# Cross-attention of a gated block on one core: scores, sums and values as eight small products side by side, with the softmax sums spread by DMA

## The chip, the core and the metric

The kernel runs on one core of one Trainium2 chip. The metric is the device time of one execution in microseconds (us). Times of whole runs are medians of several executions; everything said of single instructions comes from one profiled execution. TensorE (PE) does the matrix products, VectorE (DVE) and ScalarE (ACT) the elementwise work, GpSimd (POOL) some small elementwise work, and SyncE's queue (SP) issues every DMA of this kernel, in order.

## The reference, cut to what matters

There are 8 batches of 512 tokens with 512 features, and 64 context tokens per batch. Each batch passes through a cross-attention with 16 heads of 32 features, then through a feed-forward net with ternary weights.

```python
def xattn(hs, ctx, mask):                     # hs: layernorm(x), ctx: 64 tokens
    q, k, v = proj(hs, Wq, bq), proj(ctx, Wk, bk), proj(ctx, Wv, bv)   # 16 heads of 32
    s = clip(einsum('bhsd,bhtd->bhst', q, k) / sqrt(32), -50, 50)
    s = clip(where(attend, s, -1e4), -50, 50)
    p = softmax(s); p = p / (p.sum(-1) + 1e-8)
    c = einsum('bhst,bhtd->bhsd', p, v)        # heads side by side again
    d = rs * (c @ Wo.T + bo)
    return layernorm(d) * ln_gamma + ln_beta

x = x + tanh(g_xattn) * xattn(layernorm(x), ctx, mask)
x = x + tanh(g_ffn) * ffn(layernorm(x))        # ffn: silu(gate) * val, then out;
                                               # rows quantised to 8 bits, weights to -1, 0, 1
```

## The kernel before

Activations of the attention are 32-bit floats. A batch is cut into four token tiles of 128 (`ST`) and four feature chunks of 128 (`DC`); a chunk holds four heads. For each batch the loop at the end of `common_path` runs, chunk by chunk:

- `queries(b, o)`: four accumulating products (L236) give 128 query features of all 512 tokens, and ACT writes them to `qT` with the bias (L241).
- `scores(b, o)`: two products (L259), one for each pair of heads. The keys `kp` lie with zeros in the places of the other head, so that one product of 64 rows gives 2 heads x 64 context tokens on 128 partitions and 512 tokens along the row. ACT takes the exponential of both (L265).
- `values(b, o)`: eight products (L282). Here the probabilities are the stationary operand, 128 tokens at a time, and `vp` streams with 66 columns: 32 value features and a column of ones for each of two heads. So a softmax sum comes out beside the values, on the token's own partition. DVE takes the reciprocal (L289) and multiplies (L290) into `ctok`, which has tokens on partitions.
- `ctx_T(b, o)`: four transposes (L303) and a copy on ACT (L304) turn `ctok` into `cT`, with features on partitions, which `project_out` (L321) needs as its stationary operand.

Then come, per token tile, `project_out` with its bias, statistics and scaling on DVE (L326 to L330), and the transposes of the next batch's layernorm (`ln1`, L227, copied by ACT at L228).

The feed-forward tiles of earlier batches are set between these steps: `ffn_mid` computes half of a 128-token tile into the four PSUM banks of `psum4` (L539 for the bias rows, four products of 32 rows on four bands of the array; L544 for gate and value), ACT takes Silu (L550) and DVE multiplies (L551). `ffn_quant` finds the row maximum on DVE (L559), scales on ACT (L568), rounds on DVE (L569) and transposes through the DMA (L571). `ffn_out` (L580) multiplies by the output weights. The buffers `hq` and `hqT` hold one tile, in two halves. All other products share the four PSUM banks of `psum`. In batches 0 and 1 no feed-forward tile is there yet; between the steps stand the weights' preparation instead (`weights_step`: magnitudes L397 on ACT, ternary values L429 and L430 on DVE, each from a chunk `wraw` loaded by DMA; of `wraw` there are four buffers). After batch 7 nine tiles of the feed-forward net are left, and run alone.

Tile code is recorded in program order and then ordered for every engine by a scheduler, so that steps interleave; at run time each engine and the SP queue go through their own list in that order, and one that waits holds all that is behind it.

Of the kernel before, what the change touches and what calls it, by code (L numbers as in the profile page):

```python
# [9 lines left out]
F32 = mybir.dt.float32  # L10
# [7 lines left out]
P = 128  # L18
# [9 lines left out]
def common_path(  # L28
# [50 lines left out]
    psum = ctx.enter_context(tc.tile_pool(name="psum", bufs=4, space=bass.MemoryType.PSUM))  # L79
    psum4 = ctx.enter_context(tc.tile_pool(name="psum4", bufs=4, space=bass.MemoryType.PSUM))  # L80

    def bank():
        return psum.tile([P, NW], F32, tag="bank", name="bank")

# [12 lines left out]
    nc.gpsimd.memset(nmagic, -MAGIC)  # L97


    kp = const.tile([P, DC, B, 2, T], F32, name="kp")  # L100
    vtok = const.tile([P, CT, D], F32, name="vtok")

    vp = []
    for i in range(2):
        v = const.tile([P, NH // 2, 2, HD + 1], F32, name=f"vp{i}")
        nc.gpsimd.memset(v, 0.0)
        for hh in range(2):

            nc.gpsimd.memset(v[hh * T : (hh + 1) * T, :, hh, HD : HD + 1], 1.0 + 1e-8)
        vp.append(v)  # L110
    kv = ExitStack()
    kvp = kv.enter_context(tc.tile_pool(name="kv", bufs=1, side="right"))
    cT_in = kvp.tile([P, DC, B * T], F32, name="cT_in")
# [41 lines left out]
    attend_f = const.tile([P, B], F32, name="attend_f")  # L155
    most = const.tile([P, B], F32, name="most")

    par = const.tile([P, 2], F32, name="par")
    for q in range(2):
        nc.vector.tensor_reduce(  # L160
            par[:, q : q + 1],
            ident.rearrange("p (a q d) -> p q a d", q=2, d=HD)[:, q],
            AX.XY, ALU.add,
        )
    bkp = const.tile([P, 2, DC], F32, name="bkp")
    for q in range(2):
        nc.vector.tensor_scalar(bkp[:, q, :], bk_sb, par[:, q : q + 1], None, ALU.mult)

    def constants():
        nc.vector.tensor_copy(attend_f, mask_i)  # L170
        nc.vector.tensor_scalar(attend_f, attend_f, 0.5, None, ALU.is_gt)
# [16 lines left out]
    rs = const.tile([P, 2], F32, name="rs")  # L188

    mvall = const.tile([P, B * ST, 2], F32, name="mvall")  # L190
    ksum = const.tile([P, 2 * DC], F32, name="ksum")
    nok = const.tile([P, B], F32, name="nok")

    def rsqrt(dst, var, n=1):
# [37 lines left out]
    def queries(b, o):  # L232
        hT = st_[b, "hT"]
        ps = bank()
        for c in range(DC):
            nc.tensor.matmul(  # L236
                ps, wq_sb[:, c, o * P : (o + 1) * P], hT[:, c, :],
                start=(c == 0), stop=(c == DC - 1),
            )
        qT = work.tile([P, S], F32, tag="qT", name="qT", bufs=2)  # L240
        nc.scalar.activation(qT, ps, AF.Identity, bias=bq_sb[:, o : o + 1])  # L241
        st_[b, "qT", o] = qT

    def pair_up(b):

        src = vtok[(b % 2) * T : (b % 2 + 1) * T, b // 2, :].rearrange(
            "p (n h d) -> p n h d", h=2, d=HD
        )
        for hh in range(2):
            nc.gpsimd.tensor_copy(vp[b % 2][hh * T : (hh + 1) * T, :, hh, 0:HD], src[:, :, hh, :])  # L250

    def scores(b, o):

        qT = st_[b, "qT", o]
        pr = work.tile([P, 2, S], F32, tag="prob", name="prob", bufs=2)
        both = bank(), bank()
        for j, ps in enumerate(both):
            rows = slice(j * 2 * HD, (j + 1) * 2 * HD)
            nc.tensor.matmul(  # L259
                ps, kp[rows, o, b, :, :].rearrange("p q t -> p (q t)"), qT[rows, :],  # L260
                start=True, stop=True,
            )
        for j, ps in enumerate(both):

            nc.scalar.activation(  # L265
                pr[:, j, :], ps, AF.Exp, scale=esc[:, b : b + 1], bias=esh[:, b : b + 1]
            )
        st_[b, "pr", o] = pr

    def values(b, o):  # L270

        pr = st_[b, "pr", o]
        if o == 0:
            st_[b, "rden"] = work.tile([P, DC, 2, 2, 4], F32, tag="rden", name="rden", bufs=2)
        ctok = work.tile([P, ST, P], F32, tag="ctok", name="ctok", bufs=2)
        for half in range(2):
            ps = bank()
            pc = ps[:, : 4 * 2 * (HD + 1)].rearrange("p (t n d) -> p t n d", t=2, d=HD + 1)
            for i in range(2):
                t = half * 2 + i  # L280
                for j in range(2):
                    nc.tensor.matmul(  # L282
                        pc[:, i, 2 * j : 2 * j + 2, :],
                        pr[:, j, t * P : (t + 1) * P],
                        vp[b % 2][:, 2 * o + j, :, :],
                        start=True, stop=True,
                    )
            rden = st_[b, "rden"][:, o, half, :, :].unsqueeze(3)
            nc.vector.reciprocal(rden, pc[:, :, :, HD : HD + 1])  # L289
            nc.vector.tensor_tensor(  # L290
                ctok[:, half * 2 : half * 2 + 2, :].rearrange("p t (n d) -> p t n d", d=HD),
                pc[:, :, :, 0:HD],
                rden.to_broadcast([P, 2, 4, HD]),
                ALU.mult,
            )
        st_[b, "ctok", o] = ctok

    def ctx_T(b, o):
        ctok = st_[b, "ctok", o]
        cT = work.tile([P, S], F32, tag="cT", name="cT", bufs=DC)  # L300
        ps = bank()
        for t in range(ST):
            nc.tensor.transpose(ps[:, t * P : (t + 1) * P], ctok[:, t, :], ident)  # L303
        nc.scalar.copy(cT, ps)  # L304
        st_[b, "cT", o] = cT

    def check_sums(b):

        r = st_[b, "rden"].rearrange("p o h t n -> p (o h t n)")
        ok = work.tile([P, DC * 2 * 2 * 4], F32, tag="ok", name="ok", bufs=1)  # L310
        nc.vector.tensor_scalar(ok, r, most[:, b : b + 1], None, ALU.is_le)
        nc.vector.scalar_tensor_tensor(
            ok, r, 2e-22, ok, ALU.is_ge, ALU.mult, accum_out=nok[:, b : b + 1]
        )
# [281 lines left out]
                start=(c == 0), stop=(c == DC - 1),  # L596
            )
    for o in range(DC):
        for q in range(2):
            nc.scalar.activation(  # L600
                kp[:, o, :, q, :], kbanks[o].rearrange("p (b t) -> p b t", t=T), AF.Identity,
                scale=par[:, q : q + 1], bias=bkp[:, q, o : o + 1],
                accum_out=ksum[:, 2 * o + q : 2 * o + q + 1],
            )
    constants()
    for t in range(ST):
        ln1(0, t)
# [11 lines left out]
    stage = staging.enter_context(tc.tile_pool(name="stage", bufs=1, side="right"))  # L619
    pair_up(0)  # L620
    ternary_load("gate", gate_w, DC)
    nc.sync.dma_start(out=wo_sb, in_=wo.rearrange("(c p) o -> p c o", p=P))
    bcast(out_b, ob_bc)
    load_x(1)

    tiles = [(f, i) for f in range(B) for i in range(ST)]
    done = {"in": 0, "mid": 0, "out": 0}

    def feed_in():

        if done["in"] < len(tiles):
            ffn_in(*tiles[done["in"]])
            done["in"] += 1

    def feed(step):

        n = done["mid"]
        if step % 2 == 0:
            ffn_mid(*tiles[n], step // 2)
            return  # L640
        if step == 3:
            if n:
                ffn_out(*tiles[n - 1])
            ffn_quant(*tiles[n])
            done["mid"] += 1

    def weights_step(b, step):

        for call in {
# [15 lines left out]
        }.get((b, step), []):  # L665
            call[0](*call[1:])

    for b in range(B):


        if b > 1:
            ffn_stats(b - 2)
        if b:
            pair_up(b)
        if 0 < b < B - 1:
            load_x(b + 1)
        queries(b, 0)
        for o in range(DC):
            fed = (b == 2 and o > 1) or (b > 2 and o != 1)
            scores(b, o)  # L680
            if fed:
                feed(0)
                values(b, o)
            if o + 1 < DC:
                queries(b, o + 1)
            if not fed:
                values(b, o)
            if fed:
                feed(1)
                feed(2)  # L690
            if b > 1 and o:
                feed_in()
            ctx_T(b, o)
            if fed:
                feed(3)
            weights_step(b, o)
        if b == 0:
            sum_bounds()
        check_sums(b)
        if b + 1 < B:  # L700
            ln1_stats(b + 1)
        for t in range(ST):
            project_out(b, t)
            if b > 1:
                feed(t)
            if b + 1 < B:
                ln1(b + 1, t)
            weights_step(b, DC + t)
        add_delta(b)
        if b == 0:  # L710
            nc.vector.tensor_scalar(ob_bc, ob_bc, tg[:, 1:2], None, ALU.mult)
        if b == 1:
            nc.vector.tensor_copy(unit, gw)
            nc.vector.tensor_scalar(unit[:, 2:3], unit[:, 2:3], tg[:, 1:2], None, ALU.mult)
            staging.close()
            fp = ctx.enter_context(tc.tile_pool(name="fp", bufs=1, side="right"))
        if b > 1:
            feed_in()
        if b == B - 1:
            verdict()  # L720
    ffn_stats(B - 2)
    while done["mid"] < len(tiles):
        if tiles[done["mid"]] == (B - 2, 0):
            ffn_stats(B - 1)
        feed(0)
        feed_in()
        for step in range(1, 4):
            feed(step)
    ffn_out(B - 1, ST - 1)


@with_exitstack
def general_path(
# [576 lines left out]
```

## Time and profile before

| | us |
|---|---|
| median of 3 runs (lowest, highest) | 831.27 (828.74, 832.45) |
| the profiled execution | 836.41 |
| its span, from first to last instruction | 834.4 |
| start until the first query product, keys and values for all batches | 39.7 |
| batch 0 / batch 1, without feed-forward work (39.7 to 94.2, 94.2 to 150.3) | 54.5 / 56.1 |
| batch 2, in which the feed-forward work starts (150.3 to 245.0) | 94.7 |
| each of batches 3 to 6 | 92.2 to 92.4 |
| batch 7, without a next batch's layernorm (614.2 to 700.0) | 85.8 |
| feed-forward tiles alone (700.0 to the end) | 134.4 |

A batch is counted here from its first query product to that of the next. The profile's page gives busy shares by engine; since the parts of the kernel have different limits, the windows by batch say more than the mean.

### The profile page before, as it was taken

The page shows a single profiled execution, that of the slowest core. Times are in us where ns is not written, and L with a number is a line of the kernel's source. Part 1 is how long each engine was busy: PE and PEld are TensorE (multiplying, and loading weights), DVE is VectorE, ACT ScalarE, POOL GpSimd, SP SyncE. Part 2 cuts the span into 40 slices and gives each one's busy share as a digit, 9 for nine tenths or more (in the row PEclk, how much of TensorE's full clock was granted, in tenths as well). Part 3 has the DMA queues.
Part 4 walks back from the last instruction along what each step waited for, and adds up shares of the span by engine and source line. Part 5 has one row for each costly group of instructions (what it writes and reads, how often), then busy time and mean ns, then how long its engine had stood idle before and what let it go on. Part 6 is the DMA issues. An engine that isn't in the chain of part 4 may idle for free. (4 is left out here: it accounts for less than half of the span.)

```text
span 834.4 us, 9194 instructions
## 1 busy us (share of the span) xinstructions
PE 790.5 (95%) x3274; PEld 371.6 (45%) x3274; DVE 558.3 (67%) x1105; ACT 353.5 (42%) x435; POOL 136.3 (16%) x185
## 2 busy tenths in 40 slices
PE   7999999798999999999999999999999999999994
PEld 3445454343444544444445444444444443334441
DVE  2637787978588377765688367756786468876662
ACT  2274367334335452455344453455244442343341
POOL 1500301243013021212113021211121000300000
PEclk9997999889999999999999999999999999999998
DMA  8745041002221123222222041222222122243432
GB/s 283 237 198 202 0 162 66 1 19 39 57 57 34 38 69 45 51 64 57 57 57 60 11 102 21 49 57 58 44 45 51 32 57 45 44 83 64 88 76 55
DMA packets 106358, 59.15 MB, mean 71 GB/s; under 512 B 91712, under 2 KB 91712, under 8 KB 105280
## 3 DMA queue, kind: packets, MB, share of 16 engines
q1 hardware_dynamic: 106304, 58.49, 27.3%
q8 instruction: 27, 0.44, 0.2%
q14 instruction: 27, 0.22, 0.1%
HBM read 28.06 MB, written 8.39 MB: 44 GB/s over the span
## 5 line engine op out<-in xcount | busy, mean ns | idle before, releaser
L551 DVE SCALAR_TENSOR_TENSOR h<-four,sgv,gate 128x512 f32<-128x512 f32 x128 | 93.9, 745 | 120.5 <-PE four L544 86.4
L544 PEld LDWEIGHTS <-xqT 128*128 128x128 bf16 x1024 | 94.4, 99 | 133.0 <-issue 33.5
L550 ACT ACTIVATE gate<-four,sgv 128x512 f32<-128x512 f32 x128 | 86.1, 685 | 135.0 <-PE four L544 132.1
L544 PE MATMUL four<-gate_tern,xqT 128*128 128x512 fp8e4 x512 | 137.0, 385 | 0.3 <-DMA xqT<-xq 0.3
L544 PE MATMUL four<-val_tern,xqT 128*128 128x512 fp8e4 x512 | 133.6, 383 | 0.0
L236 PE MATMUL bank<-hT,wq_sb 128*128 128x512 f32 x256 | 124.1, 629 | 5.8 <-ACT hT L228 4.9
L580 PE MATMUL bank<-out_tern,hqT 128*128 128x512 fp8e4 x512 | 117.3, 383 | 6.4 <-DMA hqT<-hq 6.4
L568 ACT ACTIVATE h<-h,magic,h_s 128x1024 f32<-128x1024 f32 x64 | 75.9, 1233 | 104.4 <-DVE h_s L562 104.4
L321 PE MATMUL bank<-wo_sb,cT 128*128 128x512 f32 x256 | 118.5, 605 | 0.0
L580 PEld LDWEIGHTS <-hqT 128*128 128x128 bf16 x512 | 50.4, 99 | 66.6 <-DMA hqT<-hq 6.9
L236 PEld LDWEIGHTS bank<-hT,wq_sb 128*128 128x128 f32 x256 | 48.4, 199 | 68.1 <-issue 57.3
L559 DVE TENSOR_REDUCE h_g<-h 128x1 f32<-128x2048 f32 x32 | 73.1, 2286 | 1.0
L282 PEld LDWEIGHTS bank<-vp,prob 128*128 128x128 f32 x512 | 64.3, 196 | 17.0 <-ACT prob L265 8.0
L321 PEld LDWEIGHTS bank<-wo_sb,cT 128*128 128x128 f32 x256 | 47.8, 195 | 47.5 <-issue 46.3
L282 PE MATMUL bank<-vp,prob 128*128 128x66 f32 x512 | 65.8, 279 | 2.6 <-ACT prob L265 2.1
L241 ACT ACTIVATE qT<-bank,bq_sb 128x512 f32<-128x512 f32 x32 | 22.0, 687 | 108.7 <-PE bank L236 108.7
L564 POOL TENSOR_TENSOR so<-h_g,unit 128x1 f32<-128x1 f32 x32 | 7.6, 237 | 350.7 <-DVE h_g L560 350.7
L265 ACT ACTIVATE prob<-bank,esh,esc 128x512 f32<-128x512 f32 x64 | 47.3, 775 | 36.2 <-PE bank L259 36.0
L224 POOL TENSOR_TENSOR x<-x,bet_bc 128x512 f32<-128x512 f32 x32 | 41.4, 1304 | 106.3 <-DVE hs L220 69.2
L569 DVE TENSOR_SCALAR hq<-h 128x1024 bf16<-128x1024 f32 x64 | 45.2, 707 | 20.1 <-ACT h L568 20.1
L259 PE MATMUL bank<-qT,kp 64*128 64x512 f32 x128 | 49.1, 664 | 2.3 <-ACT qT L241 2.3
L539 PE MATMUL four<-brow,uT 32*128 32x512 bf16 x256 | 41.7, 386 | 5.2 <-ACT gate L550 3.5
(121 smaller groups left out, 752.0 us busy)
## 6 DMA issues: line engine op xcount, KB each, us to landing
x<-in_x SPq DMA_DIRECT2D x32, 256.0 KB, 4.7
out_x<-o SPq DMA_DIRECT2D x32, 256.0 KB, 2.2
wraw<-in_gate_w SPq DMA_DIRECT2D x4, 1024.0 KB, 8.0
wraw<-in_val_w SPq DMA_DIRECT2D x4, 1024.0 KB, 4.9
wraw<-in_out_w SPq DMA_DIRECT2D x4, 1024.0 KB, 6.5
cT_in<-in_cxT SPq DMA_DIRECT2D x4, 256.0 KB, 4.8
wk_sb<-in_wk SPq DMA_DIRECT2D x4, 256.0 KB, 5.0
wv_sb<-in_wv SPq DMA_DIRECT2D x1, 1024.0 KB, 7.4
```

The lines of the kernel that those rows point to most:

```text
L236: nc.tensor.matmul(ps, wq_sb[:, c, o * P : (o + 1) * P], hT[:, c, :], start=(c == 0), stop=(c == DC - 1),)
L259: nc.tensor.matmul(ps, kp[rows, o, b, :, :].rearrange("p q t -> p (q t)"), qT[rows, :], start=True, stop=True,)
L265: nc.scalar.activation(pr[:, j, :], ps, AF.Exp, scale=esc[:, b : b + 1], bias=esh[:, b : b + 1])
L282: nc.tensor.matmul(pc[:, i, 2 * j : 2 * j + 2, :], pr[:, j, t * P : (t + 1) * P], vp[b % 2][:, 2 * o + j, :, :], start=True, stop=True,)
L321: nc.tensor.matmul(ps, st_[b, "cT", c][:, t * P : (t + 1) * P], wo_sb[:, c, :], start=(c == 0), stop=(c == DC - 1),)
L544: nc.tensor.matmul(ps, xqT[:, c, :], w[:, c, cols], start=False, stop=(c == DC - 1))
L550: nc.scalar.activation(gate, four[2 * k], AF.Silu, scale=sgv[:, 0, i : i + 1])
L551: nc.vector.scalar_tensor_tensor(h[:, cols], four[2 * k + 1], sgv[:, 1, i : i + 1], gate, ALU.mult, ALU.mult)
L559: nc.vector.tensor_reduce(gx, h, AX.X, ALU.max, apply_absolute_value=True)
L568: nc.scalar.activation(h[:, cols], h[:, cols], AF.Identity, scale=s, bias=magic)
L569: nc.vector.tensor_scalar(hq, h[:, cols], MAGIC, None, ALU.subtract)
L580: nc.tensor.matmul(ps, hqT[:, c % (FC // 2), :], weights["out"][:, c, :], start=(c == 0), stop=(c == FC - 1),)
```

## The change

It replaces scores, values and the transposes, for two chunks (`a`, eight heads) at a time:

- `kT` holds the keys without the zeros (one eviction per chunk instead of two). `scores(b, a)` makes eight products of 32 rows by 64 columns, one per head, each on a part of the array of its own (four bands of rows, two of columns), into four banks.
- The probabilities are now the streaming operand. `sums(b, a)` makes four products of 128 rows by 32 columns with a constant `sel` and gives the eight sums, each repeated on 16 partitions. ACT copies them to `den`. A DMA writes 8 rows to DRAM (`rows`), a second reads them back as 128 x 32 (`dense`), DVE takes the reciprocal, a third DMA writes it to DRAM (`over`), and four more read it back with every row repeated on 32 partitions (`R`). All seven stand in SP's queue. `den` and `R` have one buffer.
- `values(b, a)` makes eight products of 64 rows by 32 columns into two banks; the result has features on partitions already, and DVE multiplies it by `R` straight into `cT`. There is no `ctx_T`.
- The heads come out in another order, so `wo` is loaded in six permuted pieces instead of one.
- The order of a batch's steps is written anew in three forms: `attend_alone` (batches 0 and 1), `attend_first` (batch 2), `attend` (3 to 7). `qT` has four buffers; `scores` goes to `psum4` in batches 0 and 1 and for the first half of batch 2; elsewhere it takes banks of `psum`.

```diff
-    kp = const.tile([P, DC, B, 2, T], F32, name="kp")
+    kT = const.tile([P, DC, B * T], F32, name="kT")
...
-        qT = work.tile([P, S], F32, tag="qT", name="qT", bufs=2)
+        qT = work.tile([P, S], F32, tag="qT", name="qT", bufs=DC)
...
+    def scores(b, a, pool, tag, prpool=work, prtag="prob"):
+        banks = [pool.tile([P, NW], F32, tag=tag, name=tag) for _ in range(4)]
+        for e in range(2):
+            o = 2 * a + e
+            for r, ps in enumerate(banks):
+                rows = slice(r * HD, (r + 1) * HD)
+                q = r % 2 ^ e
+                nc.tensor.matmul(
+                    ps[q * T : (q + 1) * T, :],
+                    kT[rows, o, b * T : (b + 1) * T], st_[b, "qT", o][rows, :],
+                    start=True, stop=True,
+                )
+        prs = []
+        for ps in banks:
+            pr = prpool.tile([P, S], F32, tag=prtag, name=prtag, bufs=4)
+            nc.scalar.activation(
+                pr, ps, AF.Exp, scale=esc[:, b : b + 1], bias=esh[:, b : b + 1]
+            )
+            prs.append(pr)
+        st_[b, "pr", a] = prs
+
+    def sums(b, a):
+        ps = bank()
+        for r, pr in enumerate(st_[b, "pr", a]):
+            nc.tensor.matmul(
+                ps[r * HD : (r + 1) * HD, :], sel.rearrange("p h n -> p (h n)"), pr,
+                start=True, stop=True,
+            )
+        den = work.tile([P, S], F32, tag="den", name="den", bufs=1)
+        nc.scalar.copy(den, ps)
...
+        rows = dram.tile([8, S], F32, tag="rows", name="rows")
+        nc.sync.dma_start(out=rows, in_=den[0:P:16, :])
+        dense = work.tile([P, S // 16], F32, tag="dense", name="dense", bufs=2)
+        nc.sync.dma_start(out=dense, in_=rows.rearrange("r (c n) -> (r c) n", n=S // 16))
+        nc.vector.reciprocal(rden, dense)
+        over = dram.tile([8, S], F32, tag="over", name="over")
+        nc.sync.dma_start(out=over.rearrange("r (c n) -> (r c) n", n=S // 16), in_=rden)
+        R = work.tile([P, 2, S], F32, tag="R", name="R", bufs=1)
+        for r in range(4):
+            nc.sync.dma_start(
+                out=R[r * HD : (r + 1) * HD], in_=over[2 * r : 2 * r + 2].partition_broadcast(HD)
+            )
+        st_[b, "R", a] = R
+
+    def values(b, a):
+        prs, R = st_[b, "pr", a], st_[b, "R", a]
+        banks = bank(), bank()
+        for e in range(2):
+            for r in range(4):
+                q = r % 2 ^ e
+                rows = slice(q * T, (q + 1) * T)
+                nc.tensor.matmul(
+                    banks[q][r * HD : (r + 1) * HD, :],
+                    vx[b % 2][rows, 2 * a + e, r // 2, :], prs[r][rows, :],
+                    start=True, stop=True,
+                )
+        for q, ps in enumerate(banks):
+            cT = work.tile([P, S], F32, tag="cT", name="cT", bufs=DC)
+            nc.vector.tensor_tensor(cT, ps, R[:, q, :], ALU.mult)
+            st_[b, "cT", 2 * a + q] = cT
...
+    def attend_alone(b):
+        for o in range(3):
+            queries(b, o)
+        scores(b, 0, psum4, "four")
+        weights_step(b, 0)
+        queries(b, 3)
+        sums(b, 0)
+        scores(b, 1, psum4, "four", stage, "prob2")
+        weights_step(b, 1)
+        sums(b, 1)
+        values(b, 0)
+        weights_step(b, 2)
+        values(b, 1)
+        weights_step(b, 3)
...
+    def attend(b):
+        queries(b, 0)
+        queries(b, 1)
+        tile_mid(0)
+        scores(b, 0, psum, "bank")
+        tile_mid(1)
+        sums(b, 0)
+        tile_in()
+        queries(b, 2)
+        queries(b, 3)
+        tile_out()
+        tile_mid(0)
+        values(b, 0)
+        tile_in()
+        tile_mid(1)
+        scores(b, 1, psum, "bank")
+        tile_mid(0)
+        sums(b, 1)
+        tile_in()
+        tile_mid(1)
+        tile_out()
+        tile_out()
+        values(b, 1)
+        tile_mid(0)
```

In this listing `tile_in`, `tile_mid` and `tile_out` are the feed-forward steps `ffn_in`, `ffn_mid` (with `ffn_quant` after the second half) and `ffn_out` for the next tile due. The number of feed-forward tiles done in each batch is the same as before.

## The prediction

> **What bounds the kernel now.** I read the page first, then windows by batch, then PE's timeline.
>
> ```profile
> PE 790.5 (95%) x3274; PEld 371.6 (45%) x3274; DVE 558.3 (67%) x1105; ACT 353.5 (42%) x435; POOL 136.3 (16%) x185
> 39.70:94.20 54.50, 51.33 (x182) 27.72 (x180) 32.86 (x69) 28.26 (x36) 7.79 (x8) 0.91 0.41 154
> 94.20:150.30 56.10, 50.53 (x181) 26.41 (x181) 41.53 (x75) 33.98 (x35) 6.08 (x6) 0.94 0.25 85
> 150.30:245.00 94.70, 86.49 (x332) 39.50 (x332) 72.58 (x152) 34.01 (x42) 23.13 (x29) 0.89 0.14 30
> 429.60:521.80 92.20, 91.04 (x401) 43.76 (x401) 62.99 (x129) 41.09 (x50) 16.45 (x22) 1.00 0.24 53
> ```
>
> The window columns are length, then busy time of PE, weight loads, DVE, ACT, POOL, then granted clock. In batches 3 to 6 PE is busy 91.0 of 92.2 us at full clock: nothing but less work on PE, in an order that doesn't wait, shortens them. Batches 0 to 2 already wait a little and run at 0.89 to 0.94 of the clock.
>
> What the attention products cost there (groups of one such batch):
>
> ```profile
> L282 PE MATMUL bank<-vp,prob 128*128 128x66 f32 x64 | 8.1, 275 | 0.4 <-ACT prob L265 0.2
> L259 PE MATMUL bank<-qT,kp 64*128 64x512 f32 x16 | 5.6, 641 | 0.0
> L303 PE MATMUL bank<-ident,ctok 128*128 128x128 f32 x16 | 2.7, 280 | 0.0
> ```
>
> Together 16.4. All ten PE groups of that window sum to 100.7 by the same measure against 91.04 busy (ends overlap), so these three are worth 16.4 x 0.904 = 14.8 of PE's time, and the rest 76.2.
>
> **The change, part by part.**
>
> *PE work.* Do small products run side by side? The trace shows it for bands of rows:
>
> ```profile
> 358.42 1.13 PE L259 MATMUL bank<-qT,kp 64*128 64x512 f32 x4
> 359.48 3.70 PE L236 MATMUL bank<-hT,wq_sb 128*128 128x512 f32 x8
> ...
> 405.59 0.39 PE L539 MATMUL four<-brow,uT 32*128 32x512 bf16 x4
> 405.92 1.04 PE L544 MATMUL four<-gate_tern,xqT 128*128 128x512 fp8e4 x4
> ```
>
> Each 32-bit product has two records. The two of L259, on two halves of the rows, take 1.06 from start to next start; one product of L236 takes 0.86 (3.43 for four). Four bf16 products on four bands take 0.33. No row shows bands of columns, nor eight at once. Lower bound per new group: 1.06. Upper: column bands in turn, then scores 2 x 1.06, sums 4 x 0.86, values 4 x 1.06 = 9.8 a pair of chunks. The Trainium skill ("TensorEngine Tiling (Array Packing)", Key Properties) has tiles working in parallel, but a change of tiling mode drains the array. The drain is in the 1.06 (L259 has it on both sides). I take 1.1: six groups a batch, 6.6 instead of 14.8. A steady batch's PE work becomes 76.2 + 6.6 = 82.8, so 9.4 us may be lost to waits before nothing is gained.
>
> *ACT and DVE.* Exponentials stay (64). ACT trades 32 `cT` copies (0.58) for 16 `den` copies; DVE trades 64 reciprocals (0.198) and 64 products (0.413), 39.1, for 32 products of 128x512 from PSUM (0.69, as L326) and 16 reciprocals (0.2), 25.3. Neither bounds a steady batch. The head gets four evictions of `kT` for eight of `kp`, beside PE's own work: 0.
>
> *The DMA chain.* Seven transfers after each `den`, three in sequence before `R`:
>
> ```profile
> out_x<-o SPq DMA_DIRECT2D x32, 256.0 KB, 2.2
> hqT<-hq SPq DMA_TRANSPOSE x64, 3.3
> ```
>
> The nearest row for a small lone transfer is 2.2 to landing, with 0.4 of SP per issue. Three hops 6.6, reciprocal 0.2, four `R` issues 1.6 and their landing 2.2: 10.6 from `den` to `R`, with nothing else in SP's list. Bounds: 8 (hops of 1.5) and 18 (5.0, the slowest transpose's landing). What it costs depends on where it stands.
>
> *Batch 0 (times from its first query).* PE finishes queries 0 to 2, first scores and query 3 at 15. ACT's list has the magnitudes 2 and 3 (2 x 2.1, L397) after the four exponentials and before `qT` 3, so this comes at 19.7, second scores at 20.8, their exponentials at 24, second `den` at 26. The first chain starts at 20.3, but in SP's list its `over` stands behind the second `rows` (26): `R` at 31 to 33. In DVE's list the multiplication stands behind all four ternary chunks (1.3 and 2.34 each, L429 and L430) and ends at about 41. `R` has one buffer, so the second four transfers start then; second multiplication at 46. `project_out` starts at 46 instead of 36 (75.9 - 39.7). PE idles some 20 us. **+11** with a cold clock.
>
> *Batch 1.* The same, with SP waiting for `wraw` buffers (out weights) between the hops, and DVE's `bias_rows` ahead of the reciprocal: second multiplication at 43.4 instead of 35.8. **+9** with the clock. Bounds for the two together: +12 and +35.
>
> *Batch 2.* Feed-forward work starts when DVE has finished `ffn_stats`; before at 31.9 (first L539 at 182.2), now about 28, as DVE has 4 us less before it. From there PE has six half tiles (3.85), two outputs (3.46), values 1.1, projection 13.7, transposes 1.8: 46.7, so 75; DVE has 51 of its own there. I take 85, halfway to 94.7: **-8** with some stall, bounds -18 and 0.
>
> *Batches 3 to 7.* Three waits appear that were not there:
> 1. `tile_mid(1)` now follows `scores` directly, at 11.4, but needs banks which DVE frees with L551, and DVE is in `ffn_stats` (L551 ended at 13.4 after the batch's start before, and so it does now): 1.9.
> 2. ACT's list puts the scaling (L568) of the tile just done between the first exponential of the second scores and the other three. L568 waits for DVE's maximum:
>
> ```profile
> 447.93 2.29 DVE L559 TENSOR_REDUCE h_g<-h 128x1 f32<-128x2048 f32 x1
> 451.24 2.37 ACT L568 ACTIVATE h<-h,magic,h_s 128x1024 f32<-128x1024 f32 x2 [3.14 <-DVE h_s L562]
> ```
>
> From the end of the tile's products: L551 ends 1.3 later, maximum and scale 3.1, L568 2.4, three exponentials 2.1: 8.9. PE has second scores 1.1 and half a tile 3.9 to do, then stands at `sums` for 3.9. Behind it in PE's list is the rest of the batch.
> 3. The two `tile_out` follow each other, with one tile's worth of `hqT`: the second's transposes start when the first lets go of half a buffer, and land 3.3 later. 1.2, and 0.5 for banks in between.
>
> `R` is not one of them: the first lands at about 35 where DVE wants it at 34; the second at 60 where it is wanted at 63.
>
> *The clock.* A wait costs twice if the clock drops.
>
> ```profile
> 708.67 0.38 PE L368 MATMUL bank<-chk,ones 128*128 128x1 f32 x2 [1.07 <-DVE chk L366]
> 710.60:714.20 3.60, 3.60 (x10) 1.25 (x10) 2.56 (x8) 0.69 (x1) 0.00 (x0) 0.53 0.00 0
> ```
>
> After an idle of 1.07 at 707.6 the granted clock is 0.53 from 710.6 to 714.2 with PE busy throughout: 1.7 us lost. The Trainium skill ("TensorE: Matmul & The Clock Gate", Why this matters for your kernels) asks only that no gap exceed about 3 us. By the rule wait 2 alone pays (5 x 1.7 = 8.5), by the row all three (25.5). Idles of 0.8 at 726 and 736 show no drop, so I take two per batch, 3.4.
>
> Steady batch: 82.8 + 1.9 + 3.9 + 1.2 + 0.5 + 3.4 = 93.7 against 92.2, **+1.5**, five times +7.5. The tail keeps its steps: 0.
>
> **Sum** on the profiled execution (836.4 = span 834.4 + 2.0): 836.4 + 11 + 9 - 8 + 7.5 = 855.9. The median of the runs stands at 831.3/836.4 = 0.994 of it: 850.6, called 850.
>
> **Rivals.**
> - *The waits are covered* (faster). If DVE or ACT run a little earlier than I laid them, each wait shrinks as a difference of two paths and the clock stays up. The point: the start costs 12 net, so each steady batch must lose under 9.4 - 2.4 = 7.0 to waits and clock (I have 10.9). With 3.5 lost: 836.4 + 12 - 5 x 5.9 = 818.9, or 814. For it: batches 3 to 6 hold 41 us of ACT and 63 of DVE in 92. Against: the wait at `sums` follows from the order in ACT's list.
> - *The hops are slow.* At 5.0 each, `R` comes 8.4 later; DVE, blocked at the multiplication, holds L551 and its banks: 16 chains, about half of each showing, gives 16 x 4.2 = 67 at worst, 30 to 45 where half is covered: 880 to 895.
> - *Column bands take turns.* The change then doesn't do what it says: 2 x (9.8 - 3.3) = 13 a batch more, 8 x 13 = 104: about 954. Nothing in the trace speaks for or against it for 32-bit data.
>
> **How the numbers follow.** My sum 0.45 (835 to 870); covered waits 0.23, plus 0.07 for ending within 0.5% (827.1 to 835.4, about what a measurement of this kernel can tell from no change); slow hops 0.15; columns in turn 0.10. Slower by over 0.5% is 0.45 + 0.15 + 0.10 = 0.70. The range cuts off the last case and the better part of the second below 808: 808 to 895. Both signs hold weight; the likeliest case's own range is 835 to 870.
>
> **What would show it.** Right: `sums` (L276) waiting for ACT's `prob` some 4 us in each of batches 3 to 7; PE idle of 15 us or more before the first `project_out` (L333) in batches 0 and 1; granted clock under 1 inside batches 3 to 7; groups of eight L257 and L309 of 1.0 to 1.3. Wrong: such a group at 2 or more; steady batches under 88 us; DVE's L316 waiting long for `R` in every batch; the start of batch 2 before 165.

## The result and the profile after

The changed kernel takes **864.7 us** (median of 4 runs, 855.8 to 869.9) against 831.9 beside it (828.7 to 836.5): ratio **1.035**, 95% interval 1.025 to 1.046. The ratio leaves out the execution of 869.9, which counts as slow because it is over 1.5% above the fastest, and that one is the profiled execution (span 868.1, against 836.4 and 834.4 before). Where its trace is read below for batch 5, the trace of e6 (858.9 us, the same order of steps) has the same four waits at the same places, 1.8 to 3.4 us long. The page's engine line and the windows by batch (0, 1, 2 and 5; columns as in the prediction):

```profile
PE 760.5 (88%) x3146; PEld 298.0 (34%) x3146; DVE 546.7 (63%) x1021; ACT 325.0 (37%) x399; POOL 142.1 (16%) x198
35.80:98.20 62.40, 43.45 (x166) 17.11 (x164) 40.64 (x79) 27.11 (x34) 17.43 (x12) 0.86 0.59 208
98.20:160.30 62.10, 47.59 (x165) 17.75 (x165) 37.78 (x61) 31.19 (x33) 6.52 (x8) 0.86 0.32 95
160.30:246.20 85.90, 74.50 (x317) 28.49 (x317) 71.47 (x141) 32.28 (x39) 22.78 (x30) 0.92 0.28 53
447.70:546.60 98.90, 90.42 (x384) 35.26 (x384) 61.38 (x118) 37.12 (x46) 16.81 (x23) 0.95 0.27 61
```

Every engine but POOL works less than before, and the kernel is slower. By stages, against before: head -3.9 (35.8 instead of 39.7), batch 0 +7.9, batch 1 +6.0, batch 2 -8.8, batches 3 to 6 +9.4, +7.5, +6.7 and +6.8, batch 7 with the tail +2.1: 33.7 in all. Nearly all of it is in the steady batches, as batches 3 to 7 are called here because they run one order of steps.

Do the products run side by side? The groups of batch 5:

```profile
L276 PE MATMUL bank<-prob,sel 128*32 128x512 f32 x16 | 4.5, 605 | 1.0 <-ACT prob L266 1.0
L257 PE MATMUL bank<-qT,kT 32*64 32x512 f32 x32 | 2.2, 613 | 0.0
L309 PE MATMUL bank<-prob,vx 64*32 64x512 f32 x32 | 2.2, 601 | 0.0
```

Two groups of scores are busy for 2.2 us together, and so are two of values: the eight products of one take 1.04 from start to next start (458.23 to 459.27 below), and 1.02 for values. A first group of sums takes 1.00; the 4.5 for two of them holds a stall of the second. So the saving is there. Where it goes is PE's timeline of the same batch (idle before an instruction, and what ended it, in brackets):

```profile
458.23 1.11 PE L257 MATMUL bank<-qT,kT 32*64 32x512 f32 x16
459.27 0.38 PE L551 MATMUL four<-brow,uT 32*128 32x512 bf16 x1
461.12 0.39 PE L551 MATMUL four<-brow,uT 32*128 32x512 bf16 x2 [1.47 <-DVE h L563]
462.37 0.58 PE L551 MATMUL four<-brow,uT 32*128 32x512 bf16 x1 [0.86 <-DVE h L563]
...
489.10 0.58 PE L551 MATMUL four<-brow,uT 32*128 32x512 bf16 x1 [3.06 <-DVE h L563]
...
501.52 2.38 PE L276 MATMUL bank<-prob,sel 128*32 128x512 f32 x6 [0.99 <-ACT prob L266]
...
514.63 3.63 PE L592 MATMUL bank<-out_tern,hqT 128*128 128x512 fp8e4 x16 [1.79 <-DMA hqT<-hq]
```

Four waits: 2.3 in the second half tile, 3.1 in the fourth (behind values), 3.35 at sums (499.49 to 503.84 instead of 1.00; each product starts only as its exponential ends), 1.8 at the last output. Behind the first two the clock is halved; behind the first:

```profile
461.70:468.50 6.80, 6.13 (x15) 2.03 (x15) 2.51 (x4) 2.87 (x4) 1.72 (x2) 0.50 0.00 0
```

With another 3.4 at 0.51 from 489.1 it is 10.2 us at half clock, 5.1 lost. With 0.3 at the batch's start the waits and the clock make 16.0, of which 0.3 is counted twice (most of the idle of 0.86 lies in the stretch at half clock). The work between them is the rest of 98.9, about 83.

The stall at sums is the order in ACT's list, one exponential ahead of L580 and three behind:

```profile
498.44 2.37 ACT L580 ACTIVATE h<-h,magic,h_s 128x1024 f32<-128x1024 f32 x2 [1.85 <-DVE h_s L574]
500.71 2.09 ACT L266 ACTIVATE prob<-bank,esh,esc 128x512 f32<-128x512 f32 x3
```

The wait of 3.1 was not foreseen. DVE's timeline and SP's queue there:

```profile
487.70 0.69 DVE L198 BATCH_NORM_STATS2 ln_st<-x 128x6 f32<-128x512 f32 x1 [3.87 <-DMA x<-in_x]
488.31 0.73 DVE L563 SCALAR_TENSOR_TENSOR h<-four,sgv,gate 128x512 f32<-128x512 f32 x1
...
489.77 1.29 DVE L316 TENSOR_TENSOR cT<-bank,R 128x512 f32<-128x512 f32 x2 [0.63 <-DMA R<-over]
```

```profile
471.06 0.58 SPq L287 DMA_DIRECT2D rows<-den  x1
472.82 0.33 SPq L289 DMA_DIRECT2D dense<-rows  x1
476.80 0.32 SPq L292 DMA_DIRECT2D over<-rden  x1
479.05 2.06 SPq L525 DMA_TRANSPOSE uT<-u  x1
481.21 0.52 SPq L295 DMA_DIRECT2D R<-over  x1
481.84 2.71 SPq L583 DMA_TRANSPOSE hqT<-hq  x2
484.64 0.53 SPq L128 DMA_DIRECT2D x<-in_x  x1
485.22 1.37 SPq L295 DMA_DIRECT2D R<-over  x3
```

DVE's list has statistics of an x tile of the next batch (L198) ahead of the L563 that frees a bank of `psum4`. That x load, and three of the four `R` transfers, stand in SP's list behind three transposes that hold it for 4.8 us. x lands at 487.7, `R` at 489.8, 18.7 us after its chain began: PE waits for the first, and the second is just behind.

### The profile page after: what moved, and what is told of

The parts are those of the page before. It is cut to its first block, busy times and chain, and to the rows that moved or that the text cites. A ratio compares the mean times of both kernels' runs of the same rounds, so it can differ in the third digit from the quotient of the medians.

```text
span 868.1 us, 9037 instructions
## 1 busy us (share of the span) xinstructions
PE 760.5 (88%) x3146; PEld 298.0 (34%) x3146; DVE 546.7 (63%) x1021; ACT 325.0 (37%) x399; POOL 142.1 (16%) x198
## 5 line engine op out<-in xcount | busy, mean ns | idle before, releaser
L563 DVE SCALAR_TENSOR_TENSOR h<-four,sgv,gate 128x512 f32<-128x512 f32 x128 | 94.5, 747 | 108.1 <-PE four L556 73.5
L556 PEld LDWEIGHTS <-xqT 128*128 128x128 bf16 x1024 | 98.3, 103 | 168.4 <-issue 82.0
L556 PE MATMUL four<-gate_tern,xqT 128*128 128x512 fp8e4 x512 | 149.2, 411 | 0.0
L556 PE MATMUL four<-val_tern,xqT 128*128 128x512 fp8e4 x512 | 140.5, 398 | 0.0
L592 PE MATMUL bank<-out_tern,hqT 128*128 128x512 fp8e4 x512 | 120.7, 388 | 16.8 <-DMA hqT<-hq 16.8
L333 PE MATMUL bank<-wo_sb,cT 128*128 128x512 f32 x256 | 121.4, 619 | 11.5 <-DVE cT L316 10.2
L227 PE MATMUL bank<-hT,wq_sb 128*128 128x512 f32 x256 | 114.0, 598 | 3.1 <-ACT hT L219 3.1
L580 ACT ACTIVATE h<-h,magic,h_s 128x1024 f32<-128x1024 f32 x64 | 75.9, 1232 | 85.4 <-DVE h_s L574 85.4
L592 PEld LDWEIGHTS <-hqT 128*128 128x128 bf16 x512 | 50.0, 100 | 87.6 <-DMA hqT<-hq 19.4
L551 PE MATMUL four<-brow,uT 32*128 32x512 bf16 x256 | 46.8, 395 | 37.3 <-DVE h L563 28.4
L333 PEld LDWEIGHTS bank<-wo_sb,cT 128*128 128x128 f32 x256 | 48.5, 197 | 64.5 <-issue 47.2
L500 POOL TENSOR_TENSOR x<-x,ob_bc 128x512 f32<-128x512 f32 x32 | 42.7, 1345 | 11.3 <-DVE h L497 11.2
L338 DVE TENSOR_TENSOR d<-bank,bo_bc 128x512 f32<-128x512 f32 x32 | 21.9, 684 | 34.4 <-PE bank L333 34.3
L276 PE MATMUL bank<-prob,sel 128*32 128x512 f32 x128 | 35.8, 633 | 7.8 <-ACT prob L266 7.8
L597 DVE SCALAR_TENSOR_TENSOR o<-bank,so,x 128x512 f32<-128x512 f32 x32 | 23.9, 748 | 28.9 <-PE bank L592 19.9
```

Of the source, the lines that this page charges most:

```text
L227: nc.tensor.matmul(ps, wq_sb[:, c, o * P : (o + 1) * P], hT[:, c, :], start=(c == 0), stop=(c == DC - 1),)
L333: nc.tensor.matmul(ps, st_[b, "cT", c][:, t * P : (t + 1) * P], wo_sb[:, c, :], start=(c == 0), stop=(c == DC - 1),)
L500: nc.gpsimd.tensor_tensor(xs, xs, ob_bc, ALU.add)
L551: nc.tensor.matmul(ps, uT[rows, i, :], brow[rows, jj, :], start=True, stop=False)
L556: nc.tensor.matmul(ps, xqT[:, c, :], w[:, c, cols], start=False, stop=(c == DC - 1))
L563: nc.vector.scalar_tensor_tensor(h[:, cols], four[2 * k + 1], sgv[:, 1, i : i + 1], gate, ALU.mult, ALU.mult)
```

## The experiments

**Theory.** The products shrank PE's work as costed; the loss is waits made by the order of steps, doubled in places by the clock. **Rivals:** the DMA chain costs in every batch; one resource (DVE, SP, R's single buffer) bounds the new kernel whatever the order. Lengths are from first query to first query in the profiled execution (batches 4 and 5 of one run differ by less than 2 us, but for 3.2 in e6 and 5.4 in e11); ratios are to the kernel before on the same chip.

| run | ratio (95%) | batch 0 | 1 | 2 | 4 and 5, mean |
|---|---|---|---|---|---|
| before | 1 | 54.5 | 56.1 | 94.7 | 92.3 |
| changed | 1.035 (1.025 to 1.046) | 62.4 | 62.1 | 85.9 | 99.4 |
| e1 no chain | 1.021 (1.015 to 1.026) | 54.2 | 57.6 | 85.0 | 99.0 |
| e2 x18 | 1.036 (1.029 to 1.042) | 62.5 | 58.8 | 86.4 | 99.0 |
| e3 quant late | 1.024 (1.018 to 1.029) | 62.6 | 58.9 | 85.8 | 98.6 |
| e4 out first | 1.004 (1.003 to 1.006) | 62.6 | 59.2 | 85.6 | 92.2 |
| e5 no chain, x18 | 1.025 (1.020 to 1.030) | 55.0 | 54.7 | 87.4 | 99.1 |
| e6 two R | 1.040 (1.036 to 1.044) | 62.2 | 58.9 | 86.5 | 97.8 |
| e7 order | **0.984** (0.981 to 0.986) | 62.6 | 60.7 | 85.9 | 88.8 |
| e8 POOL's queue | 1.095 (1.090 to 1.099) | 71.8 | 61.8 | 92.4 | 108.7 |
| e9 no loads | 1.037 (1.032 to 1.043) | 63.4 | 57.2 | 85.5 | 100.6 |
| e10 out in front | 0.988 (0.985 to 0.992) | 62.4 | 58.9 | 88.5 | 91.2 |
| e11 no loads, two R | (one run, 864.0) | 63.2 | 57.3 | 86.0 | 99.6 |
| e12 multiply first | 0.992 (0.988 to 0.995) | 65.9 | 61.1 | 85.8 | 89.0 |

**e1: without the chain.**

```diff
-        rows = dram.tile(...); ... seven transfers ...; R = work.tile(...)
+        nc.vector.reciprocal(rden, den[:, 0 : S // 16])
+        R = r_one   # constant tile of ones
```

> Left out: the division by the sums. The seven transfers of each chain are gone, R is a constant tile of ones, and the reciprocal reads the sums directly; all products, exponentials and steps stay. Theory (the loss sits in waits that the order of steps makes, the chain matters in batches 0 and 1 only): batches 0 and 1 shorten from 62.4 and 62.1 to 55 to 58 each, a steady batch from 99 to about 95 (the stall at sums of 3.4 and the one at the second half tile of 2.3 stay), in all 864.7 - 12 - 5 x 4 = about 833. Rival (the chain to R is what costs): steady batches fall below 88 us and the whole below 800.

849.4 us. Batches 0 and 1 return to what they were before the change, as the theory has it (54.2 and 57.6); the steady batches don't move (99.0), which both expectations missed. So the chain costs the start 12.7 us against the profiled execution of the change, and 9.2 to 11.5 against e2, e3, e4, e6, e7 and e10, whose batch 1 takes 58.8 to 60.7 and not 62.1. That it costs a steady batch nothing does not follow, as e2 shows. Without the chain `project_out` of batch 0 starts 27.5 after the batch's start (36.2 before the change), and yet the batch is as long as the old one: the saving of the products never reaches its end.

**e2: 18 buffers for x**, meant to let the x loads go early.

```diff
-            xt[t] = xpool.tile([P, D], F32, tag="x", name="x", bufs=16)
+            xt[t] = xpool.tile([P, D], F32, tag="x", name="x", bufs=18)
```

> 18 buffers for x instead of 16, so that the loads of the next batch no longer wait for a late tile_out. Theory: in a steady batch DVE then has the x tile in time, L563 isn't held behind ln1_stats, and the 3.1 us in front of L551 after values go, with 1.7 us of half clock behind them: steady batches 99 to about 94.5, in all about 842. Rival (R, which lands at the same time, takes its place in DVE's list, or the loads stay behind the chain in SP's list): under 1.5 us a batch, in all above 857.

863.1 us, as the rival had it. L198 now stands behind L563, and the wait for `R` has taken its place (DVE's timeline, batch 5):

```profile
489.02 1.29 DVE L316 TENSOR_TENSOR cT<-bank,R 128x512 f32<-128x512 f32 x2 [3.10 <-DMA R<-over]
490.23 0.74 DVE L563 SCALAR_TENSOR_TENSOR h<-four,sgv,gate 128x512 f32<-128x512 f32 x1
```

**e5: without the chain, and 18 buffers for x.**

> Left out: the division by the sums, as in the run without the chain (R is a constant tile of ones, no transfers); and 18 buffers for x. Theory (at the second half tile of a steady batch two things stand in DVE's list ahead of L563, an x tile and R, both late through SP's list, and each covers for the other): with both gone the 2.8 us in front of L551 and the half clock behind them (1.7) go: steady batches 99.0 to about 94.5, in all 847.6 - 5 x 4.5 = about 825. Rival (DVE is late for a reason of its own): steady batches stay above 97.

851.9 us, and steady batches of 99.1: my reading of e2 was incomplete. With `R` out of the way, L198 is back in front of that L563, for the x tile two further on:

```profile
480.67 0.69 DVE L200 BATCH_NORM_STATS2 ln_st<-x 128x6 f32<-128x512 f32 x1 [3.82 <-DMA x<-in_x]
481.28 0.73 DVE L555 SCALAR_TENSOR_TENSOR h<-four,sgv,gate 128x512 f32<-128x512 f32 x1
```

(L200 and L555 are this kernel's L198 and L563.) Two more buffers let every load go two outputs earlier, but it still stands right behind an output's store in SP's list, and DVE's list has the statistics of whichever tile comes in there at a place where it has not landed yet. Two late arrivals, x and `R`, stand before the same L563; neither e1, e2 nor e5 removes both, and each alone is enough for the wait. What they share is the place of `tile_out` and of the transposes ahead of them in SP's list.

**e4: the first `tile_out` of a batch ahead of its first half tile.**

```diff
         queries(b, 1)
+        tile_out()
         tile_mid(0)
...
         queries(b, 3)
-        tile_out()
         tile_mid(0)
```

> In batches 3 to 7 the first tile_out moves from behind queries 3 to behind queries 1, ahead of the first half tile. Theory: PE reaches tile_mid(1) 3.5 us later, when DVE is out of ffn_stats (2.3 us of wait and 3.4 us of half clock go), and the x loads, which wait for that tile_out, come in time (3.1 + 1.7 us go): a steady batch 99 to 90 to 92, in all 820 to 830. Rival: tile_mid(0) of the next tile, now 3.5 us closer to tile_in, waits for ffn_stats and uT instead: a steady batch stays at 97 or more.

836.0 us, 29 less by moving one line; steady batches 99.4 to 92.2, granted clock 1.00:

```profile
448.84 1.10 PE L257 MATMUL bank<-qT,kT 32*64 32x512 f32 x10 [1.59 <-DVE o L597]
472.41 1.60 PE L257 MATMUL bank<-qT,kT 32*64 32x512 f32 x12 [0.47 <-DVE cT L316]
432.20:524.00 91.80, 86.93 (x385) 34.61 (x385) 62.12 (x118) 37.01 (x46) 16.83 (x23) 1.00 0.28 67
```

Both waits on L563 and all half-clock stretches are gone from this batch: at the second half tile DVE is out of `ffn_stats`, and the output, the loads behind it and the transposes come earlier, L316 waits 1.50 for `R`, and PE is held by it for 0.5 only. A smaller new wait appears, 1.59 at the first scores, for the bank of that output (L597, behind `ffn_stats`). The rival (the next tile late) did not happen. The whole came out 6 above the expected 820 to 830, the batch at its upper end.

**e3: second scores ahead of the quantisation**, so that ACT's list has all exponentials ahead of L580.

```diff
-        tile_mid(1)
-        scores(b, 1, psum, "bank")
+        tile_mid(1, lambda: scores(b, 1, psum, "bank"))   # between ffn_mid and ffn_quant
```

> In batches 3 to 7 the second scores are emitted between the half tile and its quantisation, so all four exponentials stand ahead of L580 in ACT's list. Theory: the stall at sums (L276 on ACT prob, 3.4 us a batch) falls under 0.5, steady batches shorten by about 3, in all about 850. Rival: hqT comes 2.8 us later and the wait moves to L592 (1.8 us a batch becomes 4 to 5): no change, 862 to 867.

852.2 us, near the 850 expected, but by luck, as it does not come from the expected place. The stall at sums is gone (eight records in a row), yet batches 4 and 5 lose 0.8 only; the larger gains are batches 1 (-3.2, which the edit does not touch, and which is the profiled execution's long batch 1 again), 6 (-5.7) and 7 with the tail (-6.9). The last two were not explained. In batch 5:

```profile
495.08 1.06 PE L276 MATMUL bank<-prob,sel 128*32 128x512 f32 x8
...
507.85 5.31 PE L592 MATMUL bank<-out_tern,hqT 128*128 128x512 fp8e4 x16 [1.78 <-DMA hqT<-hq]
```

The wait for `hqT` is as long as before (1.79), but the 16 products behind it now take 5.31 instead of 3.63: the clock is halved there. With 0.9 of a new wait for ACT's Silu, and 0.3 more in front of the fourth half tile, the 3.35 are nearly spent. The rival's place, `hqT`, was right; its mechanism, a longer wait, was not.

**e7: the order put together.** e4 and e3, two buffers for `R`, and the last `tile_out` of a batch moved away from the one before it:

```diff
         tile_out()
-        tile_out()
         values(b, 1)
         tile_mid(0)
+        tile_out()
```

> Together: first tile_out ahead of the first half tile, second scores ahead of the quantisation in ACT's list, the last tile_out of a batch behind values and the half tile after it, two buffers for R. Theory (the products did shrink PE's work by 8 to 10 us a batch, and what is lost is lost to the order of steps): the waits for hqT (1.8) and at sums (1.7) go from the 91.8 of the run with tile_out first: a steady batch 87.5 to 89, batches 0 and 1 together 7 less, in all 837 - 5 x 3.5 - 7 = about 812, ratio 0.97 to 0.985. Rival (DVE or the chain then sets a batch): a steady batch stays at 91 to 92 and the whole above 828.

818.2 us, **1.6% under the kernel before** (0.981 to 0.986). The same products and the same chain as in the change; only their places differ.

```profile
426.20:514.80 88.60, 85.22 (x384) 34.31 (x384) 62.35 (x118) 36.67 (x46) 17.13 (x23) 1.00 0.30 69
```

The steady batch is where it was expected (87.5 to 89); the whole is 6 above, as batches 0 and 1 gave nothing back. By start-to-start times the work of this batch is 82.6, and 6.0 are waits, of which 4.6 lie at the scores (1.38 for L597, 0.61 for `cT`, and 2.6 inside their groups). The four edits were not run one by one on top of each other; what each gives is read from the waits that are gone.

**e10: that output in front of queries 0**, aimed at the wait for L597.

> The step order of the run that beat both, with the first tile_out of a batch moved again, in front of queries 0. Theory (the first scores wait 1.4 us, and as much inside their group, for a bank that DVE frees with L597 behind ffn_stats): the bank is asked for 6.9 us earlier, the wait goes, a steady batch 88.6 to about 86.5, in all 818 - 5 x 2 = about 808. Rival (L597 keeps its place in DVE's list behind ffn_stats, or the batch's start is now late for hqT): 817 to 822.

822.6 us, worse than e7 (the intervals just touch; batches of 91.1 against 88.8). The scores no longer wait, but the first half tile, 3.5 us earlier again, brings back the wait of the second:

```profile
444.76 0.39 PE L551 MATMUL four<-brow,uT 32*128 32x512 bf16 x2 [3.16 <-DVE h L563]
```

The gain of e4 at the second half tile is thus shown from both sides: PE must not be there before DVE leaves `ffn_stats`.

**e8: the chain on POOL's queue, 18 buffers for x.**

> The seven transfers of a chain are issued by POOL's queue instead of SP's, and x has 18 buffers; nothing is left out. Theory (SP's list, with its transposes and waits, delays R and x): R no longer waits behind uT and hqT, the wait ahead of L563 goes, a steady batch 99 to about 95. Rival: POOL, which waits in order for each hop, holds up the small operations of ffn_stats (power, u) that DVE and SP wait for: a steady batch at 100 or more.

910.3 us, the rival and worse than it: the waits at the two half tiles became 5.8 and 3.9, a new one of 3.1 for `cT` stands before L333, and the clock fell to 0.91 in that batch. POOL waits in order for each hop (107.5 us on `den` alone in the whole run), with the small operations of the statistics behind it. That this is the cause is read from these waits; no run separates it.

**e6, e9, e11: what holds batches 0 and 1.** Two buffers for `R`; the val and out weights filled by POOL instead of loaded; both.

```diff
-        R = work.tile([P, 2, S], F32, tag="R", name="R", bufs=1)
+        R = work.tile([P, 2, S], F32, tag="R", name="R", bufs=2)
```

```diff
+            if name != "gate":
+                nc.gpsimd.memset(raw, 0.01)
+                part.append(raw)
+                continue
```

> Two buffers for R instead of one. Theory (in batches 0 and 1 the second chain's last transfers wait for the first multiplication, which is late): project_out starts 4 us earlier in batch 0 (43.0 after the batch's start to about 39) and 3 to 6 earlier in batch 1 (40.4 to 35 to 37); the two batches together shorten by 5 to 9; steady batches unchanged at 99; in all about 857. Rival (DVE's ternary steps or the 1 MB weight loads set those ends): under 2 us together.

> Left out: the loads of the val and out weights (POOL fills their raw tiles with a constant instead), so that in batches 0 and 1 no transfer of 1 MB runs beside the chains; all else as changed. Theory (with R in time, DVE's four ternary chunks still hold the first multiplication of batch 0 to about 75, but the second follows at once): project_out starts 36 to 38 after the start of batch 0 instead of 43 and 35 to 37 instead of 40.4 in batch 1; each of the two batches 4 to 6 shorter; steady batches unchanged at 99. Rival (the chain's own hops or DVE set both ends): under 2 us each.

> Left out: the loads of the val and out weights (POOL fills their raw tiles with a constant); and two buffers for R. Theory (in batch 0 the second R has two causes that cover for each other: with one buffer its transfers wait for the first multiplication, with two they stand in SP's list behind weight loads and land among them): with both gone the second multiplication follows the first at once, project_out starts 38 to 39.5 after the start of batch 0 (43.0 as changed, 43.0 with two buffers, 44.1 without loads) and batch 0 lasts 58 to 60; batch 1 no longer than the 57.2 without loads. Rival (the ends are set by the chain's hops or by DVE's ternary steps): batch 0 stays at 62 or more.

Batch 0 moves with none of the three (62.2, 63.4, 63.2), so neither `R`'s buffer nor the loads hold it, alone or together; e11's theory fell. In batch 1 the loads do cost: 57.2 and 57.3 without them, 1.5 to 4.9 less than in the runs with them, and `project_out` 37.4 and 37.5 after the start instead of 39.0 to 40.9. Whether they cost by their place in SP's list or by the bandwidth that they take is not told apart; in the changed kernel four `R` transfers issued at 128.8 to 130.6 let L316 go at 137.9. DVE's timeline of the changed kernel shows this, and batch 0:

```profile
137.88 0.69 DVE L316 TENSOR_TENSOR cT<-bank,R 128x512 f32<-128x512 f32 x1 [9.26 <-DMA R<-over]
```

```profile
77.47 1.27 DVE L316 TENSOR_TENSOR cT<-bank,R 128x512 f32<-128x512 f32 x2
...
83.26 0.55 DVE L211 TENSOR_SCALAR hs<-x,ln_mv,ln_r 128x512 f32<-128x512 f32 x1 [2.96 <-PE bank L218]
83.72 1.28 DVE L316 TENSOR_TENSOR cT<-bank,R 128x512 f32<-128x512 f32 x2
```

In batch 0 the first pair waits for nothing when its turn comes: the four ternary chunks stand ahead of it until 75. The second stands behind an L211 that waits for PE's transposes (L218), which stand behind the first `project_out`.

**e12: multiplications ahead of the ternary chunks**, on e7, forced by a copy of a column of `cT` into the chunks' thresholds before these are computed.

> The step order of the run that beat both, and in batch 0 the four ternary chunks of the gate weights are held, by a copy of one column into their thresholds, until both pairs of multiplications are done. Theory (neither R's buffers nor the loads set batch 0, since taking both away left it at 63; the four chunks, 9 us of DVE ahead of the first multiplication, do): the first L316 starts 35 to 37 after the start of batch 0 instead of 42, the project_out of its last chunks about 6 earlier; DVE's evictions of project_out now stand behind the chunks, so batch 0 itself shortens by 1 to 4 of its 62.6. Rival (R itself lands after 41): L316 and the batch stay where they are. In all 812 to 818.

824.3 us; e7's 818.2 is better. The first L316 starts 33.7 after the batch's start (41.7 in e7), its `project_out` at 35.0 instead of 43.1, so the cause is the one named. But batch 0 is 3.3 longer: the first eviction of `project_out` (L338) now stands behind the chunks in DVE's list and starts when they end, at 91.3 (55.7 after the start; 52.0 in e7).
Of the two orders, the scheduler's own is the better one; a third, with the chunks spread between the projections, was not tried.

## Why the prediction was right, and where it was not

The sum gave 855.9 for the profiled execution, and 869.9 came; as a median 850 was forecast, and 864.7 came. The direction and the kind of loss were right, and the loss was larger. That it is off by no more than this is partly luck, since two errors offset each other: batches 3 to 7 with the tail cost 32.5 instead of 7.5, while head, batches 0 and 1 and batch 2 together cost 1.2 instead of 12.

- **PE's work**: predicted 1.1 a group and 82.8 a steady batch; measured 1.00 to 1.05, and 82.6 in e7. Right; the rival of bands taking turns is out, by the groups.
- **Wait 1** (second half tile, `ffn_stats`): 1.9 predicted, 2.3 measured; e4 and e10 show its cause. **Wait 2** (sums, L580): 3.9 and 3.35; e3 shows it. **Wait 3** (`hqT`): 1.7 predicted, 1.8 measured; e7 takes it away.
- **The step that failed**: "`R` is not one of them". It counted 10.6 us from `den` to `R`, SP's time for the chain included, but not the transposes that stand among its hops, and it did not ask what else SP's list makes late. The chain took 18.7, and the first `R` of batch 5 came 42.1 after the batch's start instead of about 35. x and `R` both arrive too late for a DVE list that holds L563 behind them: 3.1, and 1.7 of clock after it. This is most of the 5.2 by which the batch came out above 93.7. No run takes both late arrivals away and leaves the outputs where they are; e4, which moves what they share, takes the wait away.
- **The clock**: 3.4 predicted for two drops, 5.1 measured; the drop behind wait 1 lasted 6.8 us, not 3.4. That it belongs in the sum was right: of the two waits with a drop, the 3.06 just exceeds the 3 us of the Trainium skill ("TensorE: Matmul & The Clock Gate", Why this matters for your kernels), but wait 1 is 2.3 in two pieces, and its drop is the longer. The trace decides: the rule lets idles pass that do cost the clock here. What the drops do follow stands in the last section.
- **Batches 0 and 1**: +11 and +9 predicted, +7.9 and +6.0 measured (for batch 1, +2.7 to +4.6 in the six runs named under e1). Batch 0's first multiplication came at 41.6, predicted 41. The second was put down to `R`'s single buffer, which e6 refutes (it came at 47.7 with two, at 47.9 with one), and `project_out` does not wait for it, as its first products need the first pair only. In batch 1 the loads matter, as said. The sign "idle of 15 us before L333" held in batch 0 (15.4, at L174, which stands just before) and not in batch 1 (10.2).
- **Batch 2**: -8 predicted, -8.8 measured. The forecast was roughly the middle between two bounds, so the match is luck; no run took this batch apart.
- **The head**: 0 predicted, -3.9 measured, so the evictions were not all beside PE's own work. Before:

```profile
22.08 0.66 PE L227 MATMUL bank<-ident,hs 128*128 128x128 f32 x4 [0.86 <-DVE attend_f L171]
23.60 0.66 PE L227 MATMUL bank<-ident,hs 128*128 128x128 f32 x4 [0.86 <-ACT kp L600]
```

The transposes waited 2.0 there, of it 0.86 behind the longer row of `kp` evictions, and the clock was then 0.59 from 24.0 to 27.4; after the change the waits there are 0.3 and the clock stays up. No run separated this part.
- The start of batch 2 at 160.3 was named as a sign against the forecast (before 165); it came from the head and the smaller start, and the steady batches outweighed it.
- **The rivals**: "waits are covered" asked for under 7.0 lost to waits and clock in a steady batch. The change lost about 16; e7 loses 6.0 and is faster than before, which fits the point named there. "Slow hops" was right in what it said would follow and wrong in the reason: `R` came 8.1 later than summed, near the 8.4 of that rival, and in e2 DVE, blocked at the multiplication, held L563 and its bank. But the hops were not slow (medians of 1.8 and 1.4 to landing for `dense` and `over`; `R` 3.4, where 2.2 was taken); the transposes in SP's list were ahead of them. What `R` alone costs a steady batch stays hidden behind the x load, which makes PE wait without it (e1).
- The sign "L316 waiting long for `R` in every batch" did not come in the changed kernel: DVE waited there 14.7 us in all, 7 times in 16 chains, 9.3 of it in batch 1.

## What to carry to other kernels

Work taken off the bounding engine was worth nothing here until the other in-order lists were put in an order that keeps ahead of it: look, for each place where the bounding engine comes earlier, at what stands ahead of the instruction that releases it. When a wait stays after its apparent cause is removed, look for a second late arrival at the same instruction and move what they share (here one line, worth 29 us) instead of adding buffers to each. A stall of 2 to 3 us should be costed with the half clock that can follow it.

## What the runs showed of the hardware that I had not expected

- Eight 32-bit products on 32x64 or 64x32 tiles take 1.02 to 1.05 us together, four on 128x32 tiles 1.00.
- Whether an idle of PE drops the clock is not told by its length alone: 1.79 ahead of L592 was followed by full clock in the changed kernel and 1.78 by half clock in e3; two of 0.86 preceded 3.4 us at 0.59 in the head before, and 1.59 in e4 was followed by none. What it goes with is where the idle falls. In all 14 traces the granted clock is full or half and changes on a grid of 3.41 us (stretches at half clock last 3.41 us or a multiple). Cut along that grid, 123 of the 134 full-clock windows with PE busy for less than 40% were followed by half clock, but only 12 of the 2880 with 55% or more, and 51 of the 105 between. None of the 166 half-clock windows busy for less than 80% was followed by full clock, against 172 of the 191 above. So an idle that fills more than about half of one window costs the clock, one that is shared between two windows may not, and waits of 1.5 to 1.8 stand at the edge. Three such windows of the changed kernel; the clock is half after the first two and full after the third:

```profile
458.33:461.74 3.41, 1.72 (x19) 0.31 (x20) 2.92 (x6) 3.40 (x5) 2.75 (x3) 1.00 0.00 0
485.64:489.05 3.41, 0.41 (x11) 0.10 (x4) 1.34 (x3) 0.00 (x0) 0.00 (x0) 1.00 0.81 241
512.94:516.35 3.41, 1.72 (x8) 0.80 (x9) 2.60 (x10) 2.10 (x2) 0.19 (x1) 1.00 0.96 174
```

The row of the prediction at 707.6 is one of the 12 (its window is 69% busy by the records). No run moves an idle across the grid on purpose, so the rule is read from the traces and not tested.
- In the changed kernel a DMA transpose holds SP's queue for 1.2 us in the median and up to 2.4, a plain transfer for 0.3 to 0.6 in the median. The chain in batch 5 had `over` issued at 476.8; its first `R` was issued at 481.2, behind one transpose, and the others from 485.2, behind two more and an x load, where `over` itself lands in 1.4.
